# A four-layer graph network: 20 sorted blocks gathered in the first layer, and other panels in the layers behind it

## The chip, the cores and the metric

The kernel runs on one core of one Trainium2 chip. The metric is the device time of one execution in microseconds, the median of several runs.

## The reference

There are 6250 nodes with 256 channels and 100,000 edges (source, destination), sorted by destination. The input is normalised over its channels and cut at zero. Three layers follow, and a head of the same form; the input is added to the result.

```
def agg(h):
    return jax.ops.segment_sum(h[src], dst, num_segments=N)
for l in range(NL - 1):
    h = x + agg(x)
    h = jax.nn.relu(h @ W1s[l] + b1s[l])
    h = jax.nn.relu(h @ W2s[l] + b2s[l])
    x = h @ W3s[l] + b3s[l]
h = x + agg(x)
h = jax.nn.relu(h @ cW1 + cb1)
h = jax.nn.relu(h @ cW2 + cb2)
return h @ cW3 + cb3
```

All is float32. The sums over edges are most of the work.

## The kernel before

The nodes are cut into 49 blocks of 128 (the last has 106). The first 24 blocks (0 to 23) are sorted by degree, so that block 0 holds nodes with few edges and block 23 those with the most; these are called "s". Blocks 24 to 48 are left as they are and are called "u". The product with the first matrix is taken before the aggregation: each layer aggregates rows that are already multiplied (with w3 of one layer and w1 of the next fused), and `table{l}` in device memory holds them.

The aggregation of a block is done in one of two ways.

*Multiplied.* The block's columns of the adjacency matrix (counts, with the node itself added) are a matrix of 49 tiles of 128 x 128. TensorE multiplies all 49 tiles of `XY` (the rows, kept in the chip's memory as a high and a low part) with it. Blocks are multiplied in panels of three or four: a panel of four is 49 tiles x 4 products of 128 x 512 (line 1942, `agg<-a,XY`), one of three the same with 384 columns. ACT and DVE turn the counts of a panel from bytes to floats (`a<-at`, lines 1913 and 1915), SP loads them from `mats`, four slots to a matrix, in chunks of seven tiles (`fetch`, `at<-mat`). The order of tiles (`ORDER`) is 24 to 48, then 0 to 23.

*Gathered.* For each of a sorted block's neighbour places, one indirect transfer on POOL fetches 128 rows of the table (line 1627, `rows<-table,idxN`), and DVE adds them up in pairs (`sums`, line 1663; the first pair is copied by ACT, line 1659). In the first layer the block's own row is one gather more. Two transposes on TensorE (line 1690, `pt<-ident,u`) end a block.

In the layers 0 to 2, the blocks 0 to 18 are gathered and the other 30 multiplied; in the last one 17 and 32. The adjacency counts of 32 blocks (`seq`, the slots) are built within the first layer, beside its products: DVE writes one-hot patterns `lo` and `hi` (line 1205), TensorE multiplies them (line 1259), ACT and sometimes DVE write the counts (line 1267), SP stores a finished slot. A slot is eight such batches. `goals` spreads them so that a panel's slots are finished before the panel begins.

After a panel, or after a group of gathered blocks (`nodes_of`), two dense products and their biases follow (`mlp`, lines 1422 and 1519); the rows (`zz`, line 1524) are stored to the next table, by SP for u blocks, by an indirect transfer on POOL for each s block ("placing", line 596, with a small memset between two). Rows of the next layer are read back into `XY` as soon as a tile's last use of the layer is over (`back`, lines 1348 and 1349); those of the s blocks wait until all of them are placed. What the last panel makes goes straight from `zz` into `XY`.

The program's order is laid down by a planner that runs when the kernel is built. `clock` counts the estimated time of TensorE's instructions; `work_of(l)` is the estimated work of a layer. The gathers are spread evenly over it (`pace`), and each gather waits for the product that stands there. The pieces of `mlp` are put between products a few tiles later, in a queue, and at once ("hurry") for the last panel and block 0:

```
self.first = clock[0] + LAG
self.pace = (begun[self.l] + work_of(self.l) - CLOSE - self.first) / len(self.order)
...
queue.append(dict(steps=[seconds, thirds], first=now[0] + wait,
                  last=now[0] + wait + (0 if hurry else SPAN),
                  far=2 if hurry else far, hurry=hurry))
```

The next layer's gathers begin when all 49 blocks are stored. Which neighbours are gathered is found on the chip by `listed`, at the start of the first layer: one indirect fetch of each sorted block's edge list (line 1748, `lane<-padded,at`), then the indices (`idxN`, by way of a tile `some`).

Of the kernel before, what the change touches and what calls it, by code (L numbers as in the profile page):

```python
# [9 lines left out]
F32 = mybir.dt.float32  # L10
# [410 lines left out]
def sorted_edges(  # L421
# [42 lines left out]
    NLAYER = W1s.shape[0]  # L464
# [3 lines left out]
    NT = -(-N // P)  # L468
# [22 lines left out]
    NS = 24  # L491
    U = NT - NS
    caps = reach(E, N, NS)
    ORDER = list(range(NS, NT)) + list(range(NS))
    seq = [("u", b) for b in range(NS, NT - 3)] + [("s", b) for b in range(NS - 1, NS - 6, -1)] + [
        ("u", b) for b in range(NT - 3, NT)] + [("s", NS - 6), ("s", NS - 7)]
    early = [(0, 3)] + [(b, 4) for b in range(3, 27, 4)] + [(27, 3)]
    wide = [(b, 4) for b in range(0, 24, 4)] + [(24, 3), (27, 3)]
    final = [(b, 4) for b in range(4, 32, 4)] + [(0, 4)]
    panels = [early] + [wide] * (NLAYER - 1) + [final]  # L500
    BUILT, FIRST = len(seq), early[0][1]
    nodes_of = [[(15, 4), (11, 4), (7, 4), (4, 3), (1, 3), (0, 1)]] * NLAYER + [
        [(13, 4), (9, 4), (5, 4), (1, 4), (0, 1)]]
    KS = [sum(n for _, n in g) for g in nodes_of]
    for l in range(NLAYER + 1):
# [595 lines left out]
    with tc.manual_schedule():  # L1101
        with tc.tile_pool(name="prep", bufs=2) as prep, tc.tile_pool(
            name="ps_t", bufs=2, space=PSUM
# [607 lines left out]
        def listed(pool, ps_b):  # L1711

            pieces, G4 = [], NS // 6
            for g0 in range(0, NS, G4):
# [8 lines left out]
                shape = [P, G4, V, NS]  # L1723
                moved = pool.tile(shape, BF16, name="moved", bufs=2)
# [5 lines left out]
                g1, lane, moved = pieces.pop(0)  # L1730
# [31 lines left out]
            for b0, n in nodes_of[0]:  # L1762
                r, o = wide_of[b0], starts_of[b0]
                shape = [P, n, r]
                some = pool.tile(shape, F32, name="some", bufs=1)
                nc.vector.tensor_tensor(some, colf[:, None, :r].to_broadcast(shape),
                                        got[:, 2, b0:b0 + n, None].to_broadcast(shape), OP.is_lt)
                v = run[:, o:o + n * r].rearrange("p (n r) -> p n r", n=n)
                nc.vector.scalar_tensor_tensor(some, v, spot[:, 0:1], some, op0=OP.subtract,
                                               op1=OP.mult)  # L1770
                nc.vector.tensor_scalar(idxN[:, o:o + n * r].rearrange("p (n r) -> p n r", n=n),
                                        some, spot[:, 0:1], None, op0=OP.add)
                layers[0].listed += n
                if layers[0].listed == n:
                    layers[0].begin()
                for _ in range(5):
                    yield
# [200 lines left out]
        with tc.tile_pool(name="hots", bufs=1) as hots, tc.tile_pool(  # L1978
            name="ats", bufs=1
        ) as ats, tc.tile_pool(name="rings", bufs=AHEAD + 2) as rings, tc.tile_pool(  # L1980
            name="gath", bufs=9
        ) as gath, tc.tile_pool(name="nd", bufs=1) as nd, tc.tile_pool(
            name="ps_a", bufs=2, space=PSUM
# [36 lines left out]
def kernel(  # L2020
# [27 lines left out]
    rest = (x, src, dst, W1s, b1s, W2s, b2s, W3s, b3s, cW1, cb1, cW2, cb2, cW3, cb3, out)  # L2048
    earlier = []
    sorted_edges(tc, good, earlier, *rest)  # L2050
    done = nc.values_load(good[0:1, 0:1], min_val=0, max_val=1)
    with tc.If(done == 0):
# [27 lines left out]
```

## Time and profile before

| what | value |
|---|---|
| median of three runs | 2004.05 us (2003.39 to 2004.16) |
| the profiled execution's own time | 1999.98 us |
| its span, first to last instruction | 1998.2 us |
| mean granted TensorE clock | 0.976 |
| first gather, last gather of layer 0 | 181.8 us, 677.4 us |
| DMA, mean rate | 181 GB/s |

The page gives each engine's busy time and the chain of work that ended last. A busy share is an average over the whole span; what an edit is worth is read from the stage in which it lies. The first layer's products run from about 168 to 687 us; the layers 1 and 2 take about 440 us each behind it.

### The profile page before, as it was taken

What the parts mean: (1) busy time and instruction counts of PE and PEld (TensorE: products, weight loads), DVE (VectorE), ACT (ScalarE), POOL (GpSimd) and SP (SyncE); (2) the same over time, 40 slices, a digit from 0 to 9 for tenths busy, and PEclk for the clock granted to TensorE, in tenths of its full rate; (3) what the DMA queues carried; (4) which work ended last, traced back from release to release, by engine and by line L of the source; (5) the groups of instructions that cost most, each with busy time, mean ns of one, the idle gap of its engine ahead of it and who ended that gap; (6) DMA issues with size and microseconds to landing.
All of it is one profiled execution on the core that took longest, in us unless ns stands there. A gap on an engine that the chain in (4) does not pass through costs nothing.

```text
span 1998.2 us, 29053 instructions
## 1 busy us (share of the span) xinstructions
PE 1883.4 (94%) x9236; PEld 1471.0 (74%) x9236; DVE 1030.9 (52%) x2211; ACT 1075.0 (54%) x2166; POOL 1309.6 (66%) x1447
## 2 busy tenths in 40 slices
PE   5856999999999899999999999999999999999997
PEld 3744777777777777777789777777788777777765
DVE  7887887676756343333335443433345354343433
ACT  4745776676767564444445464444445564454442
POOL 2526766766666556777777476676777366777775
PEclk9876999999999999999999999999999999999998
DMA  5524656666656575565557575564657476665653
GB/s 167 177 75 141 202 182 191 199 199 200 208 171 215 160 233 162 173 183 168 181 179 210 160 247 175 154 194 146 196 165 236 147 217 200 186 197 175 181 175 109
DMA packets 252334, 361.40 MB, mean 181 GB/s; under 512 B 33353, under 2 KB 206313, under 8 KB 252155
## 3 DMA queue, kind: packets, MB, share of 16 engines
q1 hardware_dynamic: 188160, 190.34, 30.2%
q0 software_dynamic: 61952, 166.87, 28.0%
q10 hardware_dynamic: 2058, 2.25, 0.4%
q8 instruction: 74, 1.21, 0.2%
q14 instruction: 90, 0.73, 0.1%
HBM read 292.33 MB, written 67.40 MB: 180 GB/s over the span
## 4 chain that ended last, share of the span: by engine, by line
PE 82%; DVE 7%; DMA 5%; issue 3%; POOL 2%; ACT 1%; SPq 0%; DVEq 0%; ACTq 0%; POOLq 0%
PE agg L1942 64%; PE ps L1519 6%; PE ps L1422 6%; DMA rows<-table,idxN 3%; PE bp L1259 2%; PE bp L1050 1%; DVE ws L768 1%; DVE hi L1205 1%; POOL rows L1627 1%; PE pt L1690 1%; POOL lane L1748 1%; DVE lo L1205 1%; PE ps L1436 1%; PE ps L1482 0%; ACT a L1913 0%
## 5 line engine op out<-in xcount | busy, mean ns | idle before, releaser
L1942 PE MATMUL agg<-a,XY 128*128 128x512 f32 (+1 forms) x6272 | 1508.8, 392 | 16.0 <-DVE a L1915 7.3
L1627 POOL DMA_INDIRECT rows<-table,idxN x1121 | 1084.5, 967 | 474.6 <-PE agg L1942 202.6
L1942 PEld LDWEIGHTS agg<-a,XY 128*128 128x128 f32 x6272 | 1142.6, 189 | 249.5 <-issue 12.4
L1913 ACT CAST a<-at 128x512 fp32r<-128x512 uint8 (+1 forms) x1249 | 707.3, 601 | 235.0 <-PE agg L1942 225.7
L1663 DVE TENSOR_TENSOR sums<-sums,rows 128x512 f32<-128x512 f32 x477 | 331.7, 695 | 502.2 <-DMA rows<-table,idxN 461.3
L1915 DVE CAST a<-at 128x512 fp32r<-128x512 uint8 (+1 forms) x312 | 142.0, 460 | 166.3 <-PE agg L1942 143.3
L1267 ACT CAST at<-bp 128x392 uint16<-128x392 f32 x227 | 110.0, 488 | 127.2 <-PE bp L1259 122.0
L1422 PE MATMUL ps<-h,w 128*128 128x512 f32 (+2 forms) x336 | 135.0, 545 | 0.3 <-DVE zz L1524 0.3
L1519 PE MATMUL ps<-w,h 128*128 128x256 f32 x588 | 133.9, 379 | 0.0
L1205 DVE TENSOR_TENSOR lo<-lanes,pairs 128x512 bf16<-128x512 bf16 x256 | 106.7, 422 | 45.6 <-PE bp L1259 44.9
L1259 PEld LDWEIGHTS <-lo 128*128 128x128 bf16 x1028 | 57.0, 102 | 97.3 <-DVE lo L1205 41.4
L1259 PE MATMUL bp<-hi,lo 128*128 128x98 bf16 x1028 | 94.4, 218 | 34.5 <-DVE lo L1205 27.7
L1519 PEld LDWEIGHTS ps<-w,h 128*128 128x128 f32 x588 | 111.5, 190 | 16.0
L596 POOL DMA_INDIRECT table<-zz,ids x72 | 72.5, 1007 | 68.3 <-DVE zz L1524 49.3
L1659 ACT COPY sums<-rows 128x512 f32<-128x512 f32 x74 | 43.8, 592 | 126.4 <-DMA rows<-table,idxN 91.2
L1425 ACT ACTIVATE h<-ps,bias 128x512 f32<-128x512 f32 (+2 forms) x84 | 51.6, 636 | 96.2 <-PE ps L1422 96.1
L1422 PEld LDWEIGHTS ps<-h,w 128*128 128x128 f32 x336 | 62.9, 192 | 52.8 <-issue 37.6
L1698 ACT ACTIVATE h<-pt,bias 128x256 f32<-128x256 f32 (+1 forms) x84 | 33.0, 444 | 127.7 <-PE pt L1690 127.7
L1524 DVE TENSOR_TENSOR zz<-ps,w 128x512 f32<-128x512 f32 (+1 forms) x81 | 50.5, 638 | 96.6 <-PE ps L1519 83.2
L1349 DVE TENSOR_TENSOR XY<-back,XY 128x256 fp32r<-128x256 f32 x138 | 54.7, 422 | 46.3 <-ACT XY L1348 45.9
L1956 ACT ACTIVATE h<-agg,bias 128x512 f32<-128x512 f32 (+1 forms) x60 | 37.3, 669 | 72.5 <-PE agg L1942 72.3
L1205 DVE TENSOR_TENSOR hi<-hi,pairs 128x784 bf16<-128x784 bf16 x128 | 72.7, 568 | 4.4
(239 smaller groups left out, 957.3 us busy)
## 6 DMA issues: line engine op xcount, KB each, us to landing
at<-mat SPq DMA_DIRECT2D x140, 448.0 KB
mat<-at SPq DMA_DIRECT2D x32, 784.0 KB
at<-mat SPq DMA_DIRECT2D x62, 336.0 KB
rows<-table,idxN POOLq DMA_INDIRECT x1121
back<-table SPq DMA_DIRECT2D x138, 128.0 KB
table<-zz SPq DMA_DIRECT2D x35, 256.0 KB
at<-mat SPq DMA_DIRECT2D x63, 112.0 KB
own<-zz SPq DMA_DIRECT2D x55, 128.0 KB
```

The lines of the kernel that those rows point to most:

```text
L596: got = nc.gpsimd.indirect_dma_start(out=ap, out_offset=bass.IndirectOffsetOnAxis(ap=ids[:, b:b + 1], axis=0), in_=sb, in_offset=None)
L1205: nc.vector.tensor_tensor(o, values, which[:, :, None, :].to_broadcast(shape), op)
L1259: mm = nc.tensor.matmul(bp[:, m * HW:(m + 1) * HW], lo[:, m, :], hi[:, m, :], start=(i == 0), stop=(i == len(sets) - 1))
L1267: nc.scalar.copy(o, v)
L1349: later(1, lambda: nc.vector.tensor_tensor(XY[:, j:j + m, C:], z[:, :m, :], XY[:, j:j + m, :C].bitcast(F32), OP.subtract))
L1422: mm = nc.tensor.matmul(ps[:, :w], weights[l][0][:, c, i * P:(i + 1) * P], h1[:, c, :w], start=(c == 0), stop=(c == KC - 1))
L1519: mm = nc.tensor.matmul(o, h2[0][:, c, nodes], w3[:, c, :], start=(c == 0), stop=(c == KC - 1))
L1627: got = nc.gpsimd.indirect_dma_start(out=t[:, c % 2, :], out_offset=None, in_=tables[self.l][:, :], in_offset=bass.IndirectOffsetOnAxis(ap ...
L1663: nc.vector.tensor_tensor(sums, sums, rows.rearrange("p h c -> p (h c)"), OP.add)
L1913: nc.scalar.copy(o, v)
L1915: nc.vector.tensor_copy(o, v)
L1942: mm = nc.tensor.matmul(agg[c][:, :w], XY[:, j, o:o + P], a[:, :w], start=(i == 0 and half == 0), stop=(i == NT - 1 and half == 1))
```

## The change

The first layer gathers 20 sorted blocks (0 to 19) and multiplies 29, in panels of 3, 4, 4, 4, 4, 4, 3 and 3 blocks. Before it was 19 and 30, in panels of 3, six times 4, and 3. The gathered blocks of the first layer come in groups of 4, 4, 4, 4, 3 and 1. The slots are built in another order: nineteen u blocks, four s blocks (23 to 20), six u blocks, then 19, 18 and 17. The later layers still gather 19 blocks and multiply 30, but their panels take the slots as they lie now: four of 4, one of 3, two of 4, and 3 (before six of 4, then 3 and 3). So the last panel of the layers 1 and 2 makes the blocks 43 to 45 (before 46 to 48), and the one ahead of it 46, 47, 48 and 19 (before 21, 20 and 19). The tile `some` gets the name and the two buffers of an earlier tile, `moved`.

```
-    seq = [("u", b) for b in range(NS, NT - 3)] + [("s", b) for b in range(NS - 1, NS - 6, -1)] + [
-        ("u", b) for b in range(NT - 3, NT)] + [("s", NS - 6), ("s", NS - 7)]
-    early = [(0, 3)] + [(b, 4) for b in range(3, 27, 4)] + [(27, 3)]
-    wide = [(b, 4) for b in range(0, 24, 4)] + [(24, 3), (27, 3)]
+    seq = [("u", b) for b in range(NS, NT - 6)] + [("s", b) for b in range(NS - 1, NS - 5, -1)] + [
+        ("u", b) for b in range(NT - 6, NT)] + [("s", b) for b in range(NS - 5, NS - 8, -1)]
+    early = [(0, 3)] + [(b, 4) for b in range(3, 23, 4)] + [(23, 3), (26, 3)]
+    wide = [(b, 4) for b in range(0, 16, 4)] + [(16, 3), (19, 4), (26, 4), (23, 3)]
     final = [(b, 4) for b in range(4, 32, 4)] + [(0, 4)]
     panels = [early] + [wide] * (NLAYER - 1) + [final]
     BUILT, FIRST = len(seq), early[0][1]
-    nodes_of = [[(15, 4), (11, 4), (7, 4), (4, 3), (1, 3), (0, 1)]] * NLAYER + [
+    nodes_of = [[(16, 4), (12, 4), (8, 4), (4, 4), (1, 3), (0, 1)]] + [
+        [(15, 4), (11, 4), (7, 4), (4, 3), (1, 3), (0, 1)]] * (NLAYER - 1) + [
         [(13, 4), (9, 4), (5, 4), (1, 4), (0, 1)]]
...
-                some = pool.tile(shape, F32, name="some", bufs=1)
+                some = pool.tile(shape, F32, name="moved", bufs=2)
```

Each pair in `early`, `wide` and `final` is the first slot of a panel and its width; each pair in `nodes_of` is the first block of a gathered group and its size.

What the planner makes of it shows on POOL at the end of the first layer. Before, from the last gathers of block 3 on (`rows<-table_87` is a gather of the first layer, with `ids` the own row of a block; `table_88<-zz` places a block's rows):

```order
L1627 DMA rows<-table_87,idxN 128x256 x7
L1627 DMA rows<-table_87,ids 128x256
L1627 DMA rows<-table_87,idxN 128x256 x5
L596 DMA table_88<-zz,ids 6378x256
L594 MEMSET mark 1x4
L596 DMA table_88<-zz,ids 6378x256
L594 MEMSET mark 1x4
L596 DMA table_88<-zz,ids 6378x256
L594 MEMSET mark 1x4
L596 DMA table_88<-zz,ids 6378x256
L1627 DMA rows<-table_87,idxN 128x256 x5
L1627 DMA rows<-table_87,ids 128x256
```

Now the same place, one line further down in the file, from the placing of the blocks 4 to 7 on:

```order
L597 DMA table_88<-zz,ids 6378x256
L595 MEMSET mark 1x4
L597 DMA table_88<-zz,ids 6378x256
L595 MEMSET mark 1x4
L597 DMA table_88<-zz,ids 6378x256
L595 MEMSET mark 1x4
L597 DMA table_88<-zz,ids 6378x256
L1628 DMA rows<-table_87,idxN 128x256 x6
L1628 DMA rows<-table_87,ids 128x256
L1628 DMA rows<-table_87,idxN 128x256 x10
L1628 DMA rows<-table_87,ids 128x256
```

The four placings that stood five gathers and one own row ahead of the layer's last gather (blocks 22 to 19, multiplied) are gone from there; the last four placings now stand 18 gathers ahead of it, and those of the blocks 23 to 20 stand in the panel before.

On TensorE the second place is the step from layer 1 to layer 2. Before (`pt<-ident,u` are block 0's transposes; `x4` and `x6` products of lines 1422 and 1519 belong first to the group of blocks 1 to 3, the 128x128 one and the x2 one to block 0, the last pair to the last panel):

```order
L1422 MATMUL ps<-h_11645,w_8298 128x384 x4
L1942 MATMUL agg<-a,XY 128x384 x8
L1690 MATMUL pt<-ident,u 128x128 x2
L1942 MATMUL agg<-a,XY 128x384 x8
L1942 MATMUL agg<-a,XY 128x512 x4
L1519 MATMUL ps<-w_8300,h_11894 128x256 x6
L1942 MATMUL agg<-a,XY 128x512 x16
L1422 MATMUL ps<-h_11921,w_8298 128x128 x4
L1942 MATMUL agg<-a,XY 128x512 x8
L1519 MATMUL ps<-w_8300,h_11993 128x256 x2
L1942 MATMUL agg<-a,XY 128x512 x8
L1422 MATMUL ps<-h_11936,w_8298 128x384 x4
```

Now:

```order
L1691 MATMUL pt<-ident,u 128x128 x2
L1423 MATMUL ps<-h_11721,w_8340 128x384 x4
L1943 MATMUL agg<-a,XY 128x384 x4
L1943 MATMUL agg<-a,XY 128x512 x16
L1520 MATMUL ps<-w_8342,h_11971 128x256 x6
L1943 MATMUL agg<-a,XY 128x512 x16
L1423 MATMUL ps<-h_11968,w_8340 128x128 x4
L1943 MATMUL agg<-a,XY 128x512 x8
L1520 MATMUL ps<-w_8342,h_12062 128x256 x2
L1943 MATMUL agg<-a,XY 128x512 x8
L1423 MATMUL ps<-h_11984,w_8340 128x384 x4
```

Block 0's transposes stood behind the first dense product of blocks 1 to 3 and two tiles more, and stand ahead of it now; everything that follows comes three tiles later in the new layer.

## The prediction

> **What bounds the kernel now.** The page comes first, then busy time by stage, then the chain of work that ended last in order of time, then the gathers on POOL and the few waits of TensorE.
>
> ```profile
> span 1998.2 us, 29053 instructions
> PE 1883.4 (94%) x9236; PEld 1471.0 (74%) x9236; DVE 1030.9 (52%) x2211; ACT 1075.0 (54%) x2166; POOL 1309.6 (66%) x1447
> PE agg L1942 64%; PE ps L1519 6%; PE ps L1422 6%; DMA rows<-table,idxN 3%; PE bp L1259 2%; PE bp L1050 1%; DVE ws L768 1%; DVE hi L1205 1%; POOL rows L1627 1%; PE pt L1690 1%; POOL lane L1748 1%; DVE lo L1205 1%; PE ps L1436 1%; PE ps L1482 0%; ACT a L1913 0%
> ```
>
> TensorE holds the chain, and 64% of the span are the products with the adjacency matrix (line 1942). By stage (columns: stretch, length, then busy us of PE, PEld, DVE, ACT and POOL, then the granted clock):
>
> ```profile
> 168.00:231.00 63.00, 50.08 (x356) 41.52 (x356) 51.35 (x139) 40.06 (x98) 45.12 (x45) 0.90 0.57 171
> 231.00:296.00 65.00, 63.61 (x476) 45.61 (x476) 52.11 (x165) 45.97 (x94) 42.57 (x42) 1.00 0.60 189
> 296.00:360.00 64.00, 63.91 (x352) 45.38 (x351) 46.36 (x95) 44.64 (x92) 39.64 (x41) 1.00 0.60 192
> 640.00:700.00 60.00, 50.95 (x264) 42.91 (x262) 23.90 (x52) 32.42 (x78) 31.34 (x39) 0.94 0.55 174
> 720.00:1060.00 340.00, 340.00 (x1457) 268.79 (x1455) 137.58 (x259) 164.19 (x303) 248.02 (x268) 1.00 0.60 182
> ```
>
> Inside a layer TensorE is full (63.91 of 64 us, 340 of 340). It waits in the first panel (50.08 of 63) and where the first layer ends (50.95 of 60). So a product taken out of the middle of the first layer is worth its whole length, unless the gathers that replace it make one of those two places worse.
>
> **Products removed from the first layer.** The chain in order of time has long unbroken runs of line 1942:
>
> ```profile
> 661.73 5.62 PE agg L1942 x32
> 711.32 42.00 PE agg L1942 x180
> ```
>
> A product of 512 columns takes 42.00/180 = 0.2333 us, one of 384 columns 5.62/32 = 0.1756 us. One panel of four becomes one of three: 49 tiles x 2 halves of the channels x 2 halves of the precision = 196 products, each 0.0577 us shorter: **-11.3 us**. Two transposes of the twentieth gathered block come back (0.2 us, from the x2 row below). The dense work on 49 blocks is the same in all. ACT's casts get shorter too and are not on the path. Net -11.1 us.
>
> **Cover in the new sixth panel (counted from nought).** It is three blocks wide, and three slots (24 batches of the building) are made beside it instead of 21 batches beside four.
>
> ```profile
> L1205 DVE TENSOR_TENSOR lo<-lanes,pairs 128x512 bf16<-128x512 bf16 x175 | 73.9, 424 | 44.6 <-PE bp L1259 43.9
> L1663 DVE TENSOR_TENSOR sums<-sums,rows 128x512 f32<-128x512 f32 x106 | 73.4, 692 | 26.9 <-DMA rows<-table,idxN 21.3 <-issue 2.8 <-DMA rows<-table,ids 1.7
> L1205 DVE TENSOR_TENSOR hi<-hi,pairs 128x784 bf16<-128x784 bf16 x88 | 50.0, 568 | 3.1
> L1205 DVE TENSOR_TENSOR hi<-cols,pairs 128x784 bf16<-128x784 bf16 x87 | 48.9, 562 | 0.0
> ```
>
> The panel lasts about 64 - 11 = 53 us (296 to 360 is a panel of four). A batch takes DVE 0.424 + (0.568 + 0.562)/2 = 0.99 us, 24 of them 24 us; some 36 gathers add 18 sums of 0.692 us, 12.5 us; other work about 5 us (an estimate from the rest of that row's 46 us). That is 41.5 of 53 us, 78%. DVE was at 52.11 of 65 and 46.36 of 64 while TensorE stayed full, so I cost this at nothing.
>
> **Gathers added.** Block 19 costs 20 rows of neighbours and its own row: 21 gathers more, 330 instead of 309.
>
> ```profile
> 181.00:231.00 50.00, 29.00 (x29) 0.93 0.57 172
> 231.00:296.00 65.00, 40.14 (x40) 1.00 0.60 189
> ...
> 626.00:678.00 52.00, 28.31 (x30) 1.00 0.72 227
> sum 497.00, POOL 305.72; mean POOL 38.21
> L1627 POOL DMA_INDIRECT rows<-table,idxN x1121: 940/946/1422, 181.8 to 1973.7; - x187
> 170.09 1.10 POOL L1748 DMA_INDIRECT lane<-padded,at  x1 [0.30 <-issue]
> 171.49 0.94 POOL L1748 DMA_INDIRECT lane<-padded,at  x1 [0.30 <-issue]
> ...
> 644.95 1.01 POOL L596 DMA_INDIRECT table<-zz,ids  x1 [2.79 <-DMA back<-table]
> ...
> 664.67 0.95 POOL L1627 DMA_INDIRECT rows<-table,idxN  x1 [0.30 <-ACT a L1913]
> 665.93 1.01 POOL L596 DMA_INDIRECT table<-zz,ids  x1 [0.30 <-issue]
> ...
> 669.82 0.98 POOL L596 DMA_INDIRECT table<-zz,ids  x1 [0.22 <-issue]
> 671.11 0.98 POOL L1627 DMA_INDIRECT rows<-table,idxN  x1 [0.30 <-PE agg L1942]
> ...
> 677.41 0.95 POOL L1627 DMA_INDIRECT rows<-table,ids  x1 [0.30 <-issue]
> ```
>
> The gathers take 305.72 us of POOL (busy), 0.99 us each over 309, and at least 0.30 us between two: 1.29 us. In the 497 us from the first to the last one POOL needs 309 x 1.29 = 399, seven fetches of edge lists (line 1748, 1.3 each: 9) and 20 placings of rows (line 596, 1.3 each: 26): 434, so 63 us are free. After: 21 x 1.29 = 27 more, 11 us less time, 1.3 for one more list to fetch; 24 of 485 us stay free. POOL keeps up on the whole, but a backlog drains slower: the pace goes from 497/309 = 1.61 to 485/330 = 1.47 us a gather, so the room per gather falls from 0.32 to 0.18 us.
>
> **The start.** The lists are fetched first, and the sums on DVE, which stand ahead of the building, wait for the first rows:
>
> ```profile
> 188.39 0.70 DVE L1663 TENSOR_TENSOR sums<-sums,rows 128x512 f32<-128x512 f32 x1 [7.39 <-DMA rows<-table,idxN]
> 245.92 0.70 DVE L1663 TENSOR_TENSOR sums<-sums,rows 128x512 f32<-128x512 f32 x1 [3.56 <-DMA rows<-table,idxN]
> ```
>
> One more list pushes all of it by 1.3 us. By 245 us some 38 gathers have gone out (29, and 9 of the next 40), and at the denser pace 38 x (1 - 1.47/1.61) = 3.3 more are asked for by then: 4.3 us. DVE's waits grow by up to 5.5 us; TensorE paid for only part of such waits (13 us idle in the first panel, 1.4 in the second). I take **+2.5 us**, bounds 0 and +5.5.
>
> **The end of the first layer.** TensorE waits there for the last gather:
>
> ```profile
> 681.58 0.69 PE L1690 MATMUL pt<-ident,u 128*128 128x128 f32 x2 [7.76 <-DVE u L1681]
> 682.06 4.50 PE L1422 MATMUL ps<-h,w 128*128 128x384 f32 x8
> 704.12 2.74 PE L1422 MATMUL ps<-h,w 128*128 128x384 f32 x8
> 1124.15 0.44 PE L1690 MATMUL pt<-ident,u 128*128 128x128 f32 x2 [2.89 <-DVE u L1677]
> 1126.74 2.75 PE L1519 MATMUL ps<-w,h 128*128 128x256 f32 x12
> ```
>
> In the last panel seven placings stand ahead of the last gather, four of them (666 to 671) right before the last six. The change leaves four, earlier: -3.9 us of POOL. Against it the denser pace puts about 3 gathers more into those 50 us (+3.7), and the backlog drains slower. I take **-1 us**, bounds -3.9 and +6 (the gathers and half of the placings' 5 us moved to the panel before).
>
> The same product that takes 2.74 us at 704 took 4.50 right behind the wait: 1.7 us go with the clock (0.94 in 640 to 700). Behind the wait of 2.89 us at 1124 nothing is slow. [...]
>
> **The later layers.** Same blocks, other panels. In the last panel of layers 1 and 2 the placings ahead of the last gather fall from six to three, 20 to 19 over the layer (-1.3), but block 0's transposes now come ahead of the two products of group 1 to 3 (2.6 us) instead of behind them, so TensorE gets to its wait sooner. The wait of 2.89 becomes 2.89 + 2.6 - 1.3 = 4.2: **+1.3 us for each of two layers**, bounds -2.6 and +4. The blocks made by the last panel (now 43 to 45) are used three tiles sooner and made three tiles later by the next one: 5 tiles of 4 x 0.2333 = 4.7 us, where there were 11.
>
> ```profile
> 1142.99 2.75 PE L1519 MATMUL ps<-w,h 128*128 128x256 f32 x12
> 1146.30 1.03 DVE L1349 TENSOR_TENSOR XY<-zz,XY 128x512 fp32r<-128x512 f32 x2
> ```
>
> From the product's end (1145.7) to the last write of XY (1147.3) are 1.6 us, so 3.1 us are left: nothing. SP issues 28 more loads of chunks cut in two; ACT and DVE waited for them hardly at all. The final layer has one placing fewer near its end: nothing, +-1.3.
>
> **The sum.** -11.1 + 2.5 - 1 + 2.6 = **-7.0 us**. The profiled execution took 1999.98 us (span 1998.2 and 1.8 around it), so 1993.0 for it; the median of the three runs, 2004.05, lies 4.1 above, and the forecast against it is **1997.0 us**. The terms' bounds give it a range of its own of 1991 to 2002. About 0.2% (4 us) is what a measurement of this kernel can tell from no change.
>
> **The rivals.**
> *More than the forecast (chance 0.16).* The seven placings were the whole cause of the 7.76 us wait. It loses 3.9 us and with it the 1.7 us of clock, the start costs only its 1.3, the later layers nothing: -11.1 - 3.9 - 1.7 + 1.3 = -15.4, 1988.7 us. For it: POOL goes without a pause from 645 to 678. Against: the denser pace.
> *Given back at the waits (0.24).* The two longer waits of layers 1 and 2 pass the point between 2.89 us (no slow product) and 7.76 (1.7 us lost): +3.4, so -3.6 and 2000.4 us; with the start at its upper bound (+3.0) it is -0.6, 2003.4 us. [...]
> *Slower: POOL becomes the bound of the first layer (0.20).* The 24 us of room are 0.07 us for each of 330 gathers: from 1.36 us on, the layer ends with POOL. Single gathers take 1.1 to 1.4 us of 0.95 (maximum 1422 ns), and DVE, whose two-input operations run beside them, gets denser too. At 1.11 + 0.30 = 1.41 the layer is 330 x 0.05 = 16.5 us over: -7.0 + 16.5 - 2.5 (the start's term is the same lateness) = +7, 2011 us. Against: the median is 946 ns, and from 720 to 1060 POOL did 268 operations in 340 us, one in 1.27, with TensorE full. [...]
>
> **How the numbers follow.** Forecast 0.40, the rivals 0.16, 0.24 and 0.20. Faster by over 0.2%: forecast and first rival, and a little of the second, 0.60. Within: most of the second, 0.19. Slower: 0.21. The range runs from the first rival's time to most of the slower one: 1989 to 2009.
>
> **What would show it.** Right: on line 1942 196 products of 512 columns fewer and as many of 384 more, 330 gathers in the first layer, layer 1 starting 9 to 10 us sooner, and a wait at pt of 6 to 8 us. Wrong: DVE's waits for rows near 190 and 246 growing by over 6 us; POOL without a pause through panels 4 to 7 with gathers of 1.06 us and more; products behind the waits of layers 1 and 2 at 4 us instead of 2.7.

## The result, and the profile of the changed kernel

The changed kernel takes 2010.05 us (median of six runs, 2007.23 to 2013.23), the kernel before 2002.58 us beside it (six runs, 1998.63 to 2004.16). The ratio is 1.0039, 95% interval 1.0027 to 1.005: the change costs 7.8 us (5.4 to 10.0), where the forecast was a gain of 7. The profiled execution took 2009.0 us, 9.0 more than the one of before (1999.98).

The top of the page of the changed kernel:

```profile
span 2007.2 us, 29158 instructions
PE 1872.9 (93%) x9238; PEld 1472.9 (73%) x9238; DVE 1039.3 (52%) x2220; ACT 1068.4 (53%) x2164; POOL 1334.2 (66%) x1472
```

TensorE is busy for 10.5 us less than before (1883.4), close to the 11.1 that were counted. So the products went, and TensorE stands still for 19.5 us more. The next view says where. It is busy time by stage, first of before, then of the changed kernel (stretch, length, then busy us of PE, PEld, DVE, ACT and POOL, the granted clock, the DMA's share, GB/s). The first stretch is the first layer, up to the last product of its last panel; each later one ends where the last panel's second dense product begins (`ps<-w,h`, the row of x12 at 708.57, 1142.99 and 1582.27 in before, at 707.11, 1148.91 and 1590.06 now), so that both hold the same work.

```profile
150.00:686.95 536.95, 502.99 (x2984) 374.35 (x2984) 378.30 (x881) 359.61 (x767) 356.00 (x369) 0.97 0.61 191
708.57:1142.99 434.42, 429.69 (x1903) 347.55 (x1902) 179.50 (x349) 212.63 (x417) 302.49 (x331) 1.00 0.61 184
1142.99:1582.27 439.28, 434.17 (x1916) 351.15 (x1915) 179.15 (x349) 214.86 (x420) 303.47 (x331) 1.00 0.60 183
1582.27:1998.20 415.93, 397.71 (x1769) 305.34 (x1767) 168.95 (x330) 196.86 (x365) 290.05 (x316) 0.98 0.60 182
```

```profile
150.00:685.51 535.51, 492.99 (x2986) 373.65 (x2984) 384.60 (x891) 352.47 (x765) 378.38 (x392) 0.96 0.62 194
707.11:1148.91 441.80, 435.09 (x1916) 353.70 (x1914) 179.16 (x348) 214.44 (x419) 303.99 (x332) 0.99 0.60 181
1148.91:1590.06 441.15, 433.51 (x1916) 352.29 (x1915) 178.92 (x348) 214.89 (x419) 302.93 (x332) 1.00 0.59 181
1590.06:2007.20 417.14, 393.41 (x1757) 302.92 (x1755) 169.94 (x330) 195.57 (x362) 291.49 (x316) 0.99 0.59 180
```

There are two losses. In the first layer TensorE works 10.0 us less (502.99 to 492.99) and waits 8.6 us more (34.0 to 42.5 of the stretch), so it ends only 1.4 us sooner. The layers 1 and 2 are 7.4 and 1.9 us longer, the last one 1.2; -1.4 + 7.4 + 1.9 + 1.2 is the 9.0. A single pair of traces overstates how unequal the layers 1 and 2 are: in eight traces with the old later panels (before, and e1, e3, e4, e6, e7, e8 and e10 below) layer 1 lasts 433.6 to 436.9 us and layer 2 436.3 to 439.3; in the three with the new ones (the changed kernel, e2 and e9) 441.8 to 444.5 and 441.2 to 442.8. On the mean the new panels cost 7.7 us in layer 1 and 4.1 in layer 2. The end of the first layer scatters too: the row of x12 comes at 708.57, 709.43 and 711.07 us in three traces with the first layer of before (before, e2, e4), at 707.11 and 710.15 in two with that of the changed kernel (it and e5).

*Where the first layer waits.* TensorE's waits from 150 to 700 us (what it waited for: us in all, times, the longest), before and then now:

```profile
PE bp L1259 <- DVE lo L1205: 12.7, 14, 1.7
PE pt L1690 <- DVE u L1681: 7.8, 1, 7.8
PE bp L1259 <- ACT at L1267: 6.2, 2, 5.9
```

```profile
PE bp L1260 <- DVE lo L1206: 21.7, 25, 3.1
PE bp L1260 <- ACT at L1268: 8.7, 2, 8.2
PE pt L1691 <- DVE u L1682: 4.1, 1, 4.1
```

The wait for the last gather (`pt`) fell by 3.7 us; with the four placings ahead of it gone, that gather goes out 2.75 us sooner (674.66 instead of 677.41). But the building of the adjacency waits for DVE and ACT for 30.4 us instead of 18.9. The largest single case is at the start. ACT's timeline of the changed kernel, then TensorE's (start, length, what, in brackets the idle time before it and what ended it):

```profile
186.59 0.59 ACT L1660 COPY sums<-rows 128x512 f32<-128x512 f32 x1 [10.36 <-DMA rows<-table,idxN]
188.06 0.49 PE L1260 MATMUL bp<-hi,lo 128*128 128x98 bf16 x4 [8.23 <-ACT at L1268]
```

ACT stands for 10.36 us at the copy of the first gathered rows, which have not landed; the casts `at<-bp` are queued behind it on the same engine, and TensorE stands for them for 8.23 us, though they do not depend on any gather. Before, the same two waits were shorter:

```profile
185.83 0.59 ACT L1659 COPY sums<-rows 128x512 f32<-128x512 f32 x1 [7.80 <-DMA rows<-table,idxN]
187.29 0.49 PE L1259 MATMUL bp<-hi,lo 128*128 128x98 bf16 x4 [5.94 <-ACT at L1267]
```

TensorE's wait is 2.3 us longer, but ends only 0.8 us later (188.06 instead of 187.29), since TensorE came to it sooner. So most of the layer's loss arises behind it. The bias behind the first panel and behind the sixth (counted from one), before and then now, shows it growing:

```profile
230.65 1.05 ACT L1956 ACTIVATE h<-agg,bias 128x384 f32<-128x384 f32 x2
560.39 1.27 ACT L1956 ACTIVATE h<-agg,bias 128x512 f32<-128x512 f32 x2
```

```profile
233.10 1.05 ACT L1957 ACTIVATE h<-agg,bias 128x384 f32<-128x384 f32 x2
566.97 1.28 ACT L1957 ACTIVATE h<-agg,bias 128x512 f32<-128x512 f32 x2
```

The first panel ends 2.45 us late, the sixth 6.6.

*Where the layers 1 and 2 wait.* TensorE's timeline at the step from layer 1 to layer 2 in the changed kernel, and its clock there in pieces of 5 us:

```profile
1123.69 0.44 PE L1691 MATMUL pt<-ident,u 128*128 128x128 f32 x2 [2.22 <-DVE u L1678]
1123.97 4.44 PE L1423 MATMUL ps<-h,w 128*128 128x384 f32 x8
1144.46 2.75 PE L1423 MATMUL ps<-h,w 128*128 128x384 f32 x8
```

```profile
1120.00:1125.00 5.00, 2.78 (x14) 2.05 (x13) 3.01 (x7) 0.62 (x2) 0.97 (x2) 0.95 0.20 64
1125.00:1130.00 5.00, 5.00 (x15) 3.22 (x15) 0.78 (x2) 1.15 (x3) 0.00 (x0) 0.71 0.00 0
```

The first dense product of the blocks 1 to 3 stands behind the wait now and runs at a clock of 0.71: 4.44 us instead of the 2.75 that the same shape takes 20 us later. In before, that product ran at 1117.13, ahead of the wait, in 2.74 us.

Before did not always keep its clock there either. Behind its wait of 2.89 us at this step nothing is slow (granted clock 1.00 in the 5 us from 1125), but at the next step, from layer 2 to the last layer, it waits for 2.92 us, and the products behind that wait are slow. Its row there, and its clock:

```profile
1562.03 3.96 PE L1942 MATMUL agg<-a,XY 128*128 128x384 f32 x12
1561.00:1566.00 5.00, 4.17 (x15) 3.78 (x16) 1.70 (x4) 3.25 (x7) 0.00 (x0) 0.68 0.00 0
```

The same twelve products take 2.56 us at the step before; with the slower ones behind them before loses 1.6 us here. In seven traces with the old later panels (before, e1, e3, e4, e6, e7 and e8 below) the twelve products behind 6 of the 14 such waits took 3.66 to 4.61 us, behind the other 8 2.54 to 2.59. In the three with the new ones the first dense product was slow behind all 6: 4.11 to 5.33 us, where it takes 2.74 at other places.

### The profile page after: what moved, and what is told of

Read it like the earlier page. It is cut to its first block, busy times and chain, and to the rows that moved or that the text cites. A ratio compares the mean times of both kernels' runs of the same rounds, so it can differ in the third digit from the quotient of the medians.

```text
span 2007.2 us, 29158 instructions
## 1 busy us (share of the span) xinstructions
PE 1872.9 (93%) x9238; PEld 1472.9 (73%) x9238; DVE 1039.3 (52%) x2220; ACT 1068.4 (53%) x2164; POOL 1334.2 (66%) x1472
## 4 chain that ended last, share of the span: by engine, by line
PE 79%; DVE 8%; DMA 6%; issue 3%; POOL 2%; ACT 1%; SPq 0%; DVEq 0%; ACTq 0%; POOLq 0%
PE agg L1943 62%; PE ps L1423 6%; PE ps L1520 6%; DMA rows<-table,idxN 3%; PE bp L1260 2%; DVE hi L1206 1%; DVE ws L769 1%; DVE sums L1664 1%; DVE lo L1206 1%; PE pt L1691 1%; POOL rows L1628 1%; POOL lane L1749 1%; DMA at<-mat 1%; DMA back<-table 1%; DMA rows<-table,ids 1%
## 5 line engine op out<-in xcount | busy, mean ns | idle before, releaser
L1628 POOL DMA_INDIRECT rows<-table,idxN x1141 | 1108.2, 971 | 442.5 <-PE agg L1943 169.5
L1664 DVE TENSOR_TENSOR sums<-sums,rows 128x512 f32<-128x512 f32 x486 | 338.0, 695 | 477.7 <-DMA rows<-table,idxN 419.8
```

The costliest lines, as they stand in the source:

```text
L1628: got = nc.gpsimd.indirect_dma_start(out=t[:, c % 2, :], out_offset=None, in_=tables[self.l][:, :], in_offset=bass.IndirectOffsetOnAxis(ap ...
L1664: nc.vector.tensor_tensor(sums, sums, rows.rearrange("p h c -> p (h c)"), OP.add)
```

## The experiments

All times are compared with runs of before on the same chip. Two of the five comparisons fell on chips on which before takes 2195 us, at a granted clock of 0.94 to 0.95; they are kept apart below ("low clock"), and the explanation rests on the three others, where before takes 2002 us at 0.976, as in the result.

| run | against before | 95% interval | us |
|---|---|---|---|
| e1, first layer alone | 0.9967 | 0.9955 to 0.9979 | -6.6 |
| e2, later panels alone | 1.0053 | 1.004 to 1.0066 | +10.6 |
| e5, change, transposes later | 1.0021 | 1.0012 to 1.0031 | +4.2 |
| e6, e1 with a lead of 15 us | 0.9899 | 0.9886 to 0.9912 | -20.2 |
| e3, e1 without 19 gathers | 0.9931 | 0.9918 to 0.9944 | -13.8 |
| e4, last gathers late | 1.0013 | 1.0002 to 1.0023 | +2.6 |
| e7, lead of 15 us alone | 0.9957 | 0.9945 to 0.997 | -8.6 |
| e8, e1 with a lead of 21 us | 0.9859 | 0.9845 to 0.9874 | -28.2 |
| e9, change, lead of 21 us | 0.9934 | 0.9914 to 0.9953 | -13.2 |
| e10, e1 with a lead of 27 us | 0.9849 | 0.9836 to 0.9862 | -30.2 |

The last column is the ratio less 1, times the 2002 us of before.

### The change in two halves (e1, e2)

e1 has the first layer of the change on the old order of slots (the slot of block 19 is skipped there), and the old later panels:

```
-    early = [(0, 3)] + [(b, 4) for b in range(3, 27, 4)] + [(27, 3)]
+    early = [(0, 3)] + [(b, 4) for b in range(3, 23, 4)] + [(23, 3), (27, 3)]
...
-    nodes_of = [[(15, 4), (11, 4), (7, 4), (4, 3), (1, 3), (0, 1)]] * NLAYER + [
+    nodes_of = [[(16, 4), (12, 4), (8, 4), (4, 4), (1, 3), (0, 1)]] + [
+        [(15, 4), (11, 4), (7, 4), (4, 3), (1, 3), (0, 1)]] * (NLAYER - 1) + [
...
-                some = pool.tile(shape, F32, name="some", bufs=1)
+                some = pool.tile(shape, F32, name="moved", bufs=2)
...
-                sum(n for _, n in early[:p + 2]))
+                max(b + n for b, n in early[:p + 2]))
```

e2 has the new later panels, the same sets of blocks in the same order, on the first layer of before:

```
-    wide = [(b, 4) for b in range(0, 24, 4)] + [(24, 3), (27, 3)]
+    wide = [(b, 4) for b in range(0, 16, 4)] + [(16, 3), (22, 4), (26, 4), (19, 3)]
```

Expected of e1, and of e1 once more at the usual clock:

> The kernel before with the first layer of the changed kernel alone: 20 blocks gathered and 29 multiplied in panels of 3, five times 4, 3 and 3, while the slots keep their old order and the later layers their old panels. My theory (two separate losses: the first layer keeps only 1.4 us of the 11 us that its shorter products save, because its waits grow by 8.4 us, and the new panels of the layers 1 and 2 cost some 10 us on top): 1 to 4 us faster than before, layer 1's first gather at 711 to 714 us. Rival (the first layer's denser gathers are the whole cause, and their lateness is carried on into the later layers): 5 to 9 us slower than before.

> The same kernel as e1_first_layer, beside before once more, since the first comparison was made at a granted TensorE clock of 0.94 to 0.95 (before took 2195 us there), and the change is to be explained at 0.976. My theory (two separate losses): 1 to 4 us faster than before. Rival (the first layer's denser gathers are the whole cause, and their lateness is carried on): 5 to 9 us slower; at the lower clock it was 1.2% slower.

Expected of e2, and of e2 once more:

> The kernel before with only the panels of the layers 1 and 2 changed, to the same sets of blocks in the same order as in the changed kernel (43 to 45 last, and 46 to 48 with 19 ahead of them). The first layer is untouched. My theory: 8 to 11 us slower than before; from the last gather of layer 1 to the first of layer 2 some 36 us instead of 30.7, since the first dense product of the blocks 1 to 3 now stands behind the wait for the last gather, and the last layer, whose end hangs on POOL, hands on the late start. Rival: the 2.6 us that the prediction gave these two layers, or less.

> The same kernel as e2_later_panels, for the same reason. My theory: 8 to 11 us slower than before, with some 36 us between the last gather of layer 1 and the first of layer 2 instead of 30.7. Rival: 0 to 3 us slower.

e1 gains 6.6 us, more than the 1 to 4 that I expected, but less than the 9.6 to which the prediction's terms for the first layer add up; its layer 1's first gather comes at 712.71 us, as expected. e2 loses 10.6 us, as expected, where the prediction had 2.6; 38.5 us pass from the last gather of layer 1 to the first of layer 2, where I expected some 36. The rival, that the first layer's lateness is carried on, falls: with the first layer of the change alone the kernel is faster, and with the first layer of before untouched the later panels lose by themselves. TensorE's waits in e2 (700 to 1150 us, then 1150 to 1600), its timeline behind the first of them, and its clock there:

```profile
PE pt L1690 <- DVE u L1677: 4.9, 1, 4.9
PE ps L1422 <- DVE zz L1524: 2.4, 1, 2.4
...
PE pt L1690 <- DVE u L1677: 4.9, 1, 4.9
PE ps L1422 <- DVE zz L1524: 1.5, 1, 1.5
```

```profile
1126.47 0.69 PE L1690 MATMUL pt<-ident,u 128*128 128x128 f32 x2 [4.88 <-DVE u L1677]
1126.95 4.50 PE L1422 MATMUL ps<-h,w 128*128 128x384 f32 x8
```

```profile
1128.00:1133.00 5.00, 5.00 (x16) 3.26 (x15) 0.75 (x2) 1.11 (x3) 0.00 (x0) 0.75 0.00 0
```

The wait at `pt` is 4.88 us in both layers (2.9 before): +2.0. Counted from the last gather TensorE does not come to it sooner: it stands there 1.5 to 1.8 us after that gather went out in both kernels. The last rows are summed later. The last gather of layer 1 goes out at 1119.71 us in before and at 1119.80 in e2, and DVE's last sum of it, in before and then in e2, begins here:

```profile
1122.49 0.70 DVE L1663 TENSOR_TENSOR sums<-sums,rows 128x512 f32<-128x512 f32 x1 [1.38 <-DMA rows<-table,idxN]
```

```profile
1124.81 0.70 DVE L1663 TENSOR_TENSOR sums<-sums,rows 128x512 f32<-128x512 f32 x1 [0.59 <-DMA rows<-table,idxN]
```

That is 5.0 us behind the gather instead of 2.8 (in layer 2 4.7 instead of 2.9). In all eight traces with the old later panels it is 2.7 to 2.9 us, in the four with the new ones (the changed kernel, e2, e5, e9) 3.4 to 5.0. With three placings gone from between the last gathers, POOL sends these without a pause (in the changed kernel the last fourteen of layer 1 with 0.30 us between two); that the rows land late for this reason is my guess, and no run shows it.

The product behind the wait takes 4.50 us instead of 2.74 in layer 1: +1.8. In layer 2 this product and the twenty of line 1942 behind it (5.33 and 5.29 us instead of 2.74 and 4.88) lose 3.0, of which before lost 1.6 already: +1.4. And a wait is there that before hardly had (0.3 us in one layer): the panel of four with block 19 is the last but one now, and its first dense product waits 2.4 and 1.5 us for DVE to take an older product's result away: +1.8 on the mean. That is 6.2 us for layer 1 and 4.6 for layer 2, 10.8 for both, against 10.6 measured.

### Block 0's transposes later (e5)

The changed kernel, with block 0's transposes two tiles later in layer 1 and one in layer 2; the first dense product of the blocks 1 to 3 stands ahead of them again:

```
-                    later(2, turn)
+                    later({1: 4, 2: 3}.get(self.l, 2), turn)
```

> The changed kernel with block 0's transposes of the layers 1 and 2 two tiles and one tile later, so that the first dense product of the blocks 1 to 3 stands ahead of them again, as in before. If that order is what the new panels cost, the slow products behind the wait (4.28 us instead of 2.6) are gone in both layers, the last layer's first gather comes 3 to 6 us sooner than the changed kernel's 1596 us, and the whole is 4 to 7 us faster than the changed kernel: 1.001 +- 0.001 of before. If not (the new panels cost it elsewhere, say in the loads of chunks cut in two), within 1.5 us of the changed kernel: 1.004 of before.

It is 3.6 us faster than the changed kernel (1.0021 against 1.0039, a difference known to some 3 us), just under the 4 to 7 that were expected; the last layer's first gather, at 1594.22 us, is only 1.9 us sooner, not 3 to 6. In its trace the two transposes of block 0 come without a wait in both layers and the first dense product beside them takes 2.74 us in both (granted clock 1.00 from 1123 to 1133 us):

```profile
1125.39 2.74 PE L1423 MATMUL ps<-h,w 128*128 128x384 f32 x8
1128.89 0.38 PE L1691 MATMUL pt<-ident,u 128*128 128x128 f32 x2
```

Both layers together last 876.8 us (710.15 to 1586.93), 883.0 in the changed kernel and 873.7 before. So the order of those two pieces is 6.2 of the 9.3 us that the later panels cost in these traces, and 3.6 of e2's 10.6 by the times: a good part of it, not all.

### The first layer: gathers or panels (e3), and the lead (e6, e7, e8, e10)

e3 is e1 with 2 of the 21 gathers of block 19; 19 neighbour rows are left out of that block's sums:

```
-                    k, r = len(self.order), caps[b + i] + (l == 0)
+                    k, r = len(self.order), 2 if (l, b + i) == (0, 19) else caps[b + i] + (l == 0)
```

> e1_first_layer with 2 instead of 21 gathers for the block 19 in the first layer (19 neighbour rows are left out of that block's sums); products, panels and dense work are the same. If the denser gathers make the first layer's waits, it is 5 to 9 us faster than e1_first_layer, and layer 1's first gather comes at 704 to 708 us. If the waits come from the new panels and from where the dense products fall, it is within 2 us of e1_first_layer.

> The kernel of e3_twentieth_not_gathered for a third time (19 neighbour rows of block 19 left out in the first layer); both earlier comparisons met chips that grant a clock of 0.94 to 0.95, on which before takes 2195 us. At 0.976, if the denser gathers eat the part of the 11 us that e1_first_layer (0.9967) did not win: 0.993 to 0.995 of before, with layer 1's first gather at 705 to 710 us instead of 712.7. If the panels and the places of the dense products do: within 1.5 us of e1_first_layer.

It is 7.2 us faster than e1 (known to some 3.5), and layer 1's first gather comes at 704.91 us. So the 19 gathers by themselves cost some 7 us of the first layer, while POOL is busy for only 380 of 535 us in it. e6 is e1 with the sums planned 15 us behind their gathers instead of 9:

```
-                self.first = clock[0] + LAG
+                self.first = clock[0] + lag_of[self.l]
...
-                    self.send(int((clock[0] - self.first + LAG) / self.pace) + 1)
+                    self.send(int((clock[0] - self.first + lag_of[self.l]) / self.pace) + 1)
...
+        lag_of = [15.0] + [LAG] * NLAYER
```

e8 and e10 have 21 and 27 us there. e7 is before with the lead of 15 us and nothing else.

> e1_first_layer with the sums of the first layer 15 instead of 9 us behind their gathers. If the first layer loses its gain because DVE stands at sums whose rows are late, while the building behind them waits, DVE's idle time for rows in the first layer falls by 10 us or more and TensorE's waits for lo and hi by 4 to 8, and the kernel is 3 to 7 us faster than e1_first_layer (0.996 of before). If DVE's own work is what delays the building, it is within 1.5 us of e1_first_layer.

> The kernel of e7_lead_alone once more (before, with a lead of 15 instead of 9 us in the first layer, 19 blocks gathered). At 0.976: if the short lead is what takes back the twentieth block's gain, 5 to 10 us faster than before, and e6_longer_lead (0.9899) is 10 to 15 us faster still. If the lead mends a loss that was there already: 0.9935, 6 to 7 us from e6_longer_lead.

> The kernel of e8_lead_21 once more (20 gathered, lead 21 us). At 0.976: within 3 us of e6_longer_lead (0.9899), since DVE waits for rows for only 10 us in all there; 3 to 8 us slower than it if the nine pairs of row buffers run out.

> e8_lead_21_again with 27 instead of 21 us. The nine pairs of row buffers hold 18 gathers, some 26 us at 1.47 us each, so POOL now waits for buffers at times: within 2 us of e8_lead_21_again, or up to 5 us slower. If more lead still helps, as it did by 7.9 us from 15 to 21, 2 us or more faster.

e6 is 13.6 us faster than e1, about twice the most that I expected. DVE's, ACT's and TensorE's waits of the first layer in e1, then in e6:

```profile
DVE sums L1664 <- DMA rows<-table,idxN: 42.8, 22, 8.0
ACT sums L1660 <- DMA rows<-table,idxN: 17.7, 3, 9.4
PE bp L1260 <- DVE lo L1206: 16.8, 22, 1.7
PE bp L1260 <- ACT at L1268: 7.7, 1, 7.7
```

```profile
DVE sums L1664 <- DMA rows<-table,idxN: 9.8, 5, 3.9
ACT sums L1660 <- DMA rows<-table,idxN: 2.9, 1, 2.9
PE bp L1260 <- DVE lo L1206: 13.0, 12, 2.8
```

The two engines wait for rows for 12.7 us instead of 60.5, and TensorE's wait for `at` is gone. The first layer by stage, one row each for e1, e3, e7, e6, e8 and e10:

```profile
150.00:684.60 534.60, 494.51 (x2986) 375.78 (x2986) 384.77 (x892) 353.29 (x766) 380.07 (x391) 0.96 0.62 195
```

```profile
150.00:677.07 527.07, 491.72 (x2991) 373.54 (x2988) 380.64 (x884) 353.13 (x768) 358.24 (x372) 0.96 0.61 193
```

```profile
150.00:678.09 528.09, 501.65 (x2984) 375.10 (x2984) 379.65 (x880) 358.94 (x766) 356.78 (x369) 0.97 0.62 194
```

```profile
150.00:666.83 516.83, 492.07 (x2982) 374.03 (x2982) 384.70 (x890) 352.63 (x765) 381.41 (x391) 0.96 0.65 202
```

```profile
150.00:664.42 514.42, 490.63 (x2994) 372.73 (x2994) 387.69 (x897) 352.55 (x768) 381.20 (x392) 0.97 0.65 203
```

```profile
150.00:656.74 506.74, 485.70 (x2982) 369.40 (x2982) 384.87 (x890) 351.69 (x766) 380.29 (x392) 0.98 0.66 206
```

Length less PE busy is TensorE's idle time. With 9 us of lead it is 34.0 with 19 blocks gathered (before), 35.4 with all but 19 rows of the twentieth (e3), and 40.1 with twenty (e1). With 15 us it is 26.4 with nineteen (e7) and 24.8 with twenty (e6): the twentieth block costs no waits any more. The times say the same: e7 to e6 is 11.6 us (known to 3.6), all of the 11.1 that the products are worth; before to e1 was 6.6 (known to 2.4). So the short lead takes back part of the twentieth block's gain, as the first expectation for e7 had it, with both its numbers; and it cost 8.6 us in before already. From 15 to 21 us the time falls by another 8 us, against my expectation of 3 at most; from 21 to 27 by 2, within the intervals. The row buffers did not run out in a way that shows.

### The last gathers late (e4)

```
-                self.first = clock[0] + LAG
+                self.first = clock[0] + LAG + 6 * (self.l == NLAYER)
```

> The kernel before, with the gathers of the last layer begun about 6 us later and spread over what remains; nothing else is moved. My theory that the last layer's end hangs on POOL, which has no room left from about 1700 us on: 4 to 6 us slower than before, with the first gather of that layer at about 1595 instead of 1589 us. Rival (TensorE sets the end, and the gathers catch up): within 1.5 us of before.

> The kernel of e4_last_gathers_late for a third time (the last layer's gathers begun 6 us later). If POOL sets the end: 1.002 to 1.003 of before at 0.976. If TensorE does: less than 1.5 us.

It costs 2.6 us (0.4 to 4.6), between the two. POOL in that trace, at the last gather of layer 2, the first of the last layer, and the thirteenth:

```profile
1562.31 0.95 POOL L1627 DMA_INDIRECT rows<-table,idxN  x1 [0.30 <-PE ps L1422]
...
1594.28 0.97 POOL L1627 DMA_INDIRECT rows<-table,idxN  x1 [13.05 <-PE agg L1942]
...
1613.88 0.94 POOL L1627 DMA_INDIRECT rows<-table,idxN  x1 [0.91 <-ACT a L1913]
```

Counted from the second dense product of layer 2's last panel (1585.65 us here, 1582.27 in before), the first gather of the last layer comes 1.5 us later than in before (8.6 us instead of 7.1), the thirteenth 5.6 us later (28.2 instead of 22.6), the last one 1.9 (393.3 instead of 391.4), and the end 2.0 (418.0 instead of 415.9). So POOL has room and catches up most of the delay, and about a third of it is left at the end; whether that part gets there by way of POOL stays open. In the changed kernel the last layer is 1.2 us longer (stages above).

### The change with its first layer mended (e9)

The changed kernel with 21 us of lead in the first layer, by the same lines as e6.

> The changed kernel with only the lead of the first layer's gathers set to 21 us (e8_lead_21_again has the same lead, the slots in their old order and the old later panels, and took 0.9859 of before). If the change loses its gain in just the two ways found, the short lead and the later panels (10.6 us, e2_later_panels_again), it takes 0.991 to 0.992 of before. If the new order of the slots costs the first layer something too (the changed kernel is 3.8 us slower than the sum of e1_first_layer_again and e2_later_panels_again), 0.993 to 0.994.

0.9934 (0.9914 to 0.9953) lies in the second range, but the interval reaches the first. Two sums miss by about the same: e1 and e2 add up to +4.0 us where the change has +7.8, and e8 and e2 to 0.9912 where e9 has 0.9934. In the traces e9's first layer ends 4.0 us later than that of e8, which has the same lead and the old order (the row of x12 at 689.95 and 685.99 us). So the new order of the slots may cost the first layer some 4 us; that is little more than such traces scatter, no run compares the two orders side by side, and it stays open.

### The comparisons at the low clock

e1, e2, e3 and e4 were at 1.0122, 1.0022, 1.0019 and 1.0013 in the first of them. In the second, e3 was at 1.0025, e4 at 1.0019, and e7 and e8 had these expectations:

> The kernel of e3_twentieth_not_gathered once more (19 neighbour rows of block 19 left out in the first layer), at the usual clock if the chip grants it. e1_first_layer took 0.9967 of before there. If the denser gathers eat the part of the 11 us that e1_first_layer did not win, it is 3 to 8 us faster than e1_first_layer: 0.993 to 0.995 of before, with layer 1's first gather at 705 to 710 us instead of 712.7. If the panels and the places of the dense products do, it is within 1.5 us of e1_first_layer.

> The kernel of e4_last_gathers_late once more. In six traces so far the end came 408.8 to 412.5 us after the last layer's first gather. If POOL sets that end, gathers begun 6 us later move it by 4 to 6 us (1.002 to 1.003 of before); if TensorE does, by less than 1.5 us.

> The kernel before with only the longer lead of e6_longer_lead (15 instead of 9 us between a gather of the first layer and its sum), 19 blocks gathered as before. e6_longer_lead took 0.9899 of before, 13.6 us less than e1_first_layer. If the short lead is what takes back the gain of the twentieth block, the lead alone brings less here (309 gathers have more room each): 5 to 10 us, and 20 blocks gathered bring 10 to 15 us on top of it. If the lead mends a loss that was there already, it brings its 13 us here too, 0.9935, and the twentieth block's part stays at 6 to 7 us.

> e6_longer_lead with 21 instead of 15 us. DVE waits for rows in the first layer for only 10 us in all in that trace, so little is left to gain: within 3 us of e6_longer_lead. If the nine pairs of row buffers run out (21 us are some 14 gathers), POOL's gathers wait for buffers, and it is 3 to 8 us slower than e6_longer_lead.

e7 was at 1.0017 and e8 at 1.0148 (1.0122 to 1.0173). e1 and e8, which gain 6.6 and 28 us at 0.976, lose 27 and 32 there; e7, which gains 8.6, loses 4, and e2 loses 5 instead of 10.6. So what is said above holds for the usual clock alone. The page of e2 at the low clock shows what is different, TensorE's idle time before its main products (the last two numbers, all of it and the largest part):

```profile
L1942 PE MATMUL agg<-a,XY 128*128 128x512 f32 (+1 forms) x6272 | 1572.3, 401 | 113.1 <-issue 82.5
```

82.5 us of stalls have no releaser in the trace, and the mean product takes 401 ns; at 0.976 the same kernel has 14.4 us of idle time there in all, and 392 ns. The 19 gathers, 7 us at the usual clock, are worth 22 there (e1 2222.7 us, e3 2200.05); what makes them so dear is open.

## Why the prediction was wrong

The forecast was 1997.0 us, 7 us faster; it was 7.8 us slower, and the time of 2010.05 lies above the range. Of the 14.8 us between the two, the first layer holds 3.0 (it gains 6.6 in e1, where its terms had 9.6) and the later panels 8.0 (they cost 10.6 in e2, where I had 2.6); 3.8 are in neither run, and may belong to the new order of the slots. The terms' bounds, added up, reach to 2012 us; the 2002 that I gave for them does not follow.

- **Products removed, -11.1 us: right.** PE's busy time fell by 10.5 us over the span and by 10.0 in the first layer; and with the waits mended (e7 to e6) the gain is 11.6.
- **The start, +2.5 us: right in size, by luck.** The first panel ends 2.45 us later (its bias at 233.10 instead of 230.65 us). I named DVE's sums, but their two waits near 190 and 246 us became shorter (5.26 and 2.89 us instead of 7.39 and 3.56). The wait that grew was ACT's, at the copy of the first pair of rows; TensorE came out of it 0.8 us late, and the other 1.7 us arose behind it.
- **Cover in the middle, nothing: wrong.** This step failed for the first layer. I asked for cover in the new panel of three blocks (the seventh, counted from one) alone, compared DVE's work with its length (78% busy) and took that for cover. What mattered here is the order on DVE and ACT: a sum whose rows had not landed held the building behind it (ACT stood for 10.36 us at the first copy, TensorE for 8.23 us for the casts behind it), however much room the engine had on the mean. The two engines did not wait longer for rows (55.2 us in all, 57.9 before), but TensorE's waits for `lo` and `at` grew from 18.9 to 30.4 us. In the new panel of three it was idle for 2.5 us, where before had 0.3 in the panel of four at its place. The panels ahead of it, for which I had no term, lost more: from the first to the sixth another 4.1 us (566.97 instead of 560.39 us at the sixth, +6.6, with +2.5 of it there already). e6 and e7 show that the lead, not POOL's room or DVE's load, is the term.
- **The end of the first layer, -1 us: the named wait fell by 3.7 us,** near its better bound of -3.9, but waits for `lo` of 3.6 us stood in the same panel, where before had none, and TensorE was idle there for 9.3 us instead of 8.1. Over the last two panels it was idle for 11.8 us instead of 8.4: +3.4, not -1.
- **The later layers, +1.3 us each: wrong by the most.** The term was mis-sized. I saw that block 0's transposes move ahead of the product, and gave that 1.3 us for the longer wait alone. e2 measured 5.3 us a layer: 2.0 for the wait (4.88 us; I had 4.2), some 1.6 for the clock behind it, which I left to a rival, and 1.8 for a wait on `zz` in the panel ahead that I did not look for. The wait grew in another way than I said: counted from the last gather TensorE came no sooner, but the rows of that gather were summed 2 us later behind it, and the three placings fewer, which I counted as 1.3 us less, did not shorten the wait. The order of dense pieces around the last two panels had to be priced piece by piece.
- **XY of 43 to 45, nothing: right.** No product waits for `XY` in layers 1 to 2 of the changed kernel.
- **SP's loads of chunks cut in two, nothing: within 3 us.** TensorE's waits for `a` in layer 1 are 4.3 us instead of 1.7, in layer 2 1.6 instead of 1.7.
- **The last layer, 0 +- 1.3: right** (+1.2).

Of the rivals, *given back at the waits* named one part of what the later layers lose, the clock, and priced that part about right (3.4 us; 3.2 in e2), but not the rest: 6.0 us with the forecast's 2.6, of 10.6. Its condition, a wait longer than some point between 2.89 and 7.76 us, was wrong (see below). *Slower: POOL becomes the bound of the first layer* gives 2011 us, next to what was measured, but for a cause that did not happen: POOL is busy for 378 of 535.5 us, a gather of the first layer takes 996 ns on the mean (991 before), and the first layer's last gather goes out at 674.66 us, sooner than before (677.41). With DVE denser, busy for 384.60 of 535.51 us instead of 378.30 of 536.95, a gather takes 5 ns more; the mean of 1.11 us in that rival's sum is not reached.

On the clock, *given back at the waits* took it that a single wait had to pass some point. In the changed kernel the product behind a wait of 2.22 us was slow (4.44 us instead of 2.75, at a clock of 0.71); in before the products behind one of 2.89 us were not (the twelve in 2.56 us, the rows of x12 in 2.75, at 1.00), but those behind one of 2.92 us were (the twelve in 3.96 us, at 0.68). I had read only the first of these two in before, so that rival's +3.4 us counted a loss that before had at one step of the two. In the seven traces with the old later panels the products were slow behind 6 waits of 1.91 to 3.09 us, and not behind 8 of 1.36 to 3.25 us. So the price was a chance at each step, in before as well, and not a point to be passed; what decides it at a step, no run shows.

## What to carry to other kernels

When work of one kind is queued on an engine ahead of work of another kind, as ACT's copy of rows stood for 10.36 us ahead of its casts, ask how far its inputs are ahead, not how busy the engine is: here six to twelve more microseconds between a gather and its sum were worth 14 to 22 us, and decided whether one more gathered block gains 11.6 us or 6.6. An edit that changes a table of panels changes the steps between layers too; price each dense piece that moves past a wait, with the clock behind it (here 4.44 us at 0.71 instead of 2.75), before the gain in the middle is counted. Of the kernels run here e10 is the fastest, 0.9849 of before (30 us) at the usual clock; at the low clock the like of it (e8) was slower than before.

## What the runs showed of the hardware that I had not expected

- Twelve products of 384 columns took 4.13 us behind a wait of 1.91 us (e8) and 2.59 behind one of 3.25 (e3): at such lengths the length of a wait alone does not tell. Behind all four waits of over 3.5 us at these steps (4.76 in the changed kernel, 4.88 twice in e2, 4.28 in e9) the first dense product took 4.11 to 5.33 us instead of 2.74; the granted clock was 0.78 (1566 to 1571 us) behind the first of them and 0.75 (1128 to 1133) behind the second.
- The same kernel, before, takes 2002 us on one chip and 2195 on another, with a mean clock of 0.975 and 0.946, and an edit that gains 1.4% on the first (e8) loses 1.5% on the second.
